# Two mixture layers in one kernel: slots of 128 rows with a fixed expert, or of two 64-row halves with an expert each

## The chip, the cores and the metric

The kernel runs on one core of one Trainium2 chip. The metric is the device time of one execution in microseconds (us); the runs shown of the kernel before are 1005.9 (median of three, 1003.83 to 1006.94). One more execution was recorded by the hardware profiler, and all durations below come from it.

The core has five engines with a queue of instructions each: TensorE (PE, matmuls; its weight loads are shown as PEld), VectorE (DVE), ScalarE (ACT), GpSimd (POOL, which here issues the indirect DMAs) and SyncE (SP, which issues most other DMAs). They wait for each other through semaphores. SBUF is the working memory of 128 partitions, PSUM the memory that matmuls write.

## The reference

2048 tokens (8 sequences of 256) of 512 numbers pass through two layers, everything in f32. The parts that the change touches are the two mixtures of experts, in which each token goes to 2 of 8 experts:

```python
# layer 0, after attention (the kernel uses one 512x512 matrix per expert)
logits = jnp.clip(xt @ gate_w.T, -50.0, 50.0)
top_w, top_idx = jax.lax.top_k(logits, TOP_K)
rw = jax.nn.softmax(top_w, axis=-1)
...
contrib = jax.ops.segment_sum((xg * vals).T, rows, num_segments=H)
out = xt @ W.T + contrib.T

# layer 1, after a linear layer with adapters
probs = jax.nn.softmax(x @ gate_w, axis=-1)
gate_score, gate_idx = jax.lax.top_k(probs, TOP_K)
gate_score = gate_score / jnp.sum(gate_score, axis=-1, keepdims=True)
...
h = jnp.einsum('th,ehi->eti', x, fc1_w) + fc1_b[:, None, :]
h = jax.nn.gelu(h, approximate=False)
y = jnp.einsum('eti,eih->eth', h, fc2_w) + fc2_b[:, None, :]
out = jnp.einsum('eth,te->th', y, combine)
```

So each layer has 4096 (token, expert) rows, and how many fall to each expert is known only at run time.

## The kernel before

The kernel does attention first (q, k, v products, a gathered cache, scores, L1176 to L1240), then the mixture of layer 0, the linear layer of layer 1 with its adapters (L1581 to L1632), and the mixture of layer 1. The instructions are written out for the whole program; a scheduler places them on each engine's queue, by priorities and by what they depend on, except where `keep_in_program_order` fixes an order. `in_a_row` keeps a list of matmuls together on PE.

**Slots.** A mixture is computed in slots of 128 rows, each of one expert. An expert with n rows takes n / 128 slots, rounded up, so at most 39 slots are needed (`NSLOT`). 36 of them (`NLIKELY`) always run; the last three stand in a branch that is taken when more than 36 are in use (L1543, L1755, with the number loaded at L306).

**Routing.** `top2` and a softmax give the chosen experts `sel` and the coefficients `coef` as tables over 16 groups of 128 tokens. `route` then works on DVE and PE: ranks of each row within its expert (matmuls pst, pn, prk, L143 to L151), the number of slots per expert (nb, boff, bend), for each token the two rows that it gets (row, rows), slot and place in the slot, and the expert of each slot (owner_i). The table of tokens per slot comes out of 32 small matmuls (pm, L250) of one-hot tables: hot (L243) and put (L221 to L233), both from DVE. Results are token_i, weight and owner_i. `routing_constants` makes the tables of constants that this needs, with iotas on POOL and conversions on DVE (L95 to L133); those of layer 1 are made right before the slots of layer 0 start.

**A slot of layer 0** (L1527): POOL gathers 128 rows by an indirect DMA (`fetched`, L328), three slots ahead; PE transposes them (`turned`, L341, pa) two slots ahead, and DVE copies them to SBUF (xsT, L343). Then four matmuls, one per 128 of the 512 inputs, with xsT as the stationary operand and the expert's matrix, 512 columns, as the moving one. Which expert it is stands in a register, which PE loads from owner_i for eight slots at a time (L316), with one register operation per matmul. ACT scales by weight (L1537), and POOL adds the rows to sums_d in memory by an indirect DMA (L348).

**A slot of layer 1**: gather and transposes as above; first product ph (L1697) with w1, a copy to SBUF (h, ACT, L1705), four transposes (pu, L1711), four Gelus with the bias b1 (hs, ACT, L1714), second product py (L1725) with w2, the bias b2 added on DVE (L1733), scaled (L1736), and added to the output (L348). In PE's queue the first product of slot s is followed by the second product of slot s-1, then the transposes of h of slot s and of the gathered rows of slot s+2. PE, ACT and DVE each hold the expert's number in registers.

In the attention, po (L1230) is a pair of products in which each writes 64 of the 128 partitions of one PSUM tile:

```python
in_a_row(
    lambda c=c, r=r: nc.tensor.matmul(
        po[r * HD : (r + 1) * HD, :],
        kvs[t + c][:, v0 + r * HD : v0 + (r + 1) * HD],
        pTs[r][:, c * P : (c + 1) * P],
...
    for c in range(3)
    for r in range(2)
)
```

Names used below: the outer product of layer 1's linear layer, pc (L1623), runs on PE beside the routing of layer 1; output_rows (ph, L402) beside that of layer 0; pgb (L1396) and pw (L1348) belong to the folding of the adapters.

Of the kernel before, what the change touches and what calls it, by code (L numbers as in the profile page):

```python
# [19 lines left out]
P = 128  # L20
# [12 lines left out]
NSLOT = 2 * N // P + E - 1  # L33
NLIKELY = (2 * N + E * P // 2) // P
# [15 lines left out]
HEAD_ORDER = [0, 2, 1, 3, 4, 6, 5, 7]  # L50


@with_exitstack
def two_layer_kernel(ctx: ExitStack, tc: tile.TileContext, io: dict, out: bass.AP):
# [35 lines left out]
    def routing_constants(pool, late=False):  # L90
# [43 lines left out]
        return earlier, ahead, same_e, below_e, count, tok, part  # L134

    def route(keep, pool, psum, consts, sel, coef, tag, beside=None):


        earlier, ahead, same_e, below_e, count, tok, part = consts
        flat_sel = sel.rearrange("p i e -> p (i e)")  # L140

# [9 lines left out]
        nc.tensor.matmul(prk2, tot.to_broadcast([P, P]), ahead, start=False, stop=True)  # L151
        nb_i = pool.tile([P, E], I32, name="nb_i")
        nc.vector.tensor_scalar(nb_i, pn, float(P - 1), None, ALU.add)
        nc.vector.tensor_scalar(nb_i, nb_i, 7, None, ALU.arith_shift_right)
# [10 lines left out]
        nc.vector.tensor_scalar(boff, boff, float(P), 1.0, ALU.mult, ALU.add)  # L165
        row = pool.tile([P, NT, E], F32, name="row")
        nc.vector.tensor_tensor(
            row, prk, boff[:, None, :].to_broadcast([P, NT, E]), ALU.add
        )
        nc.vector.tensor_tensor(row, row, sel, ALU.mult)  # L170

        rows = pool.tile([P, 2, NT], F32, name="rows")
# [3 lines left out]
        cf = pool.tile([P, 2, NT], F32, name="cf")  # L176
# [8 lines left out]
        rows_i = pool.tile([P, 2, NT], I32, name="rows_i")  # L185
        nc.vector.tensor_scalar(rows_i, rows, 1.0, None, ALU.subtract)
        rem_i = pool.tile([P, 2, NT], I32, name="rem_i")
        nc.vector.tensor_scalar(rem_i, rows_i, P - 1, None, ALU.bitwise_and)
        nc.vector.tensor_scalar(rows_i, rows_i, 7, None, ALU.arith_shift_right)
        rem = pool.tile([P, 2 * NT], F32, name="rem")  # L190
        nc.vector.tensor_copy(rem, rem_i.rearrange("p r i -> p (r i)"))
        slot = pool.tile([P, 2 * NT], F32, name="slot")
        nc.vector.tensor_copy(slot, rows_i.rearrange("p r i -> p (r i)"))
# [7 lines left out]
        ge = pool.tile([P, NSLOT, E], F32, name="ge", tag="wide")  # L201
        nc.vector.tensor_tensor(
            ge,
            count[:, :NSLOT, None].to_broadcast([P, NSLOT, E]),
            bend[:, None, :].to_broadcast([P, NSLOT, E]),
            ALU.is_ge,
        )
        owner = pool.tile([P, NSLOT], F32, name="owner")
        nc.vector.tensor_reduce(owner, ge, AX.X, ALU.add)
        owner_i = keep.tile([P, NSLOT], I32, name=f"owner_i_{tag}")  # L210
        nc.vector.tensor_scalar(owner_i, owner, float(E - 1), None, ALU.min)

        used_i = keep.tile([P, 1], I32, name=f"used_i_{tag}")
        nc.vector.tensor_copy(used_i, bend[:, E - 1 :])

        if beside:
            beside()

        full = [P, 2 * NT, NSLOT]
        put = pool.tile([P, 2 * NT, 2, NSLOT], F32, name="put", tag="wide")  # L220
        nc.vector.tensor_tensor(  # L221
            put[:, :, 0, :],
            slot[:, :, None].to_broadcast(full),
            count[:, None, :NSLOT].to_broadcast(full),
            ALU.is_equal,
        )
        nc.vector.tensor_tensor(
            put[:, :, 1, :],
            put[:, :, 0, :],
            cf.rearrange("p r i -> p (r i)")[:, :, None].to_broadcast(full),  # L230
            ALU.mult,
        )
        nc.vector.tensor_tensor(  # L233
            put[:, :, 0, :],
            put[:, :, 0, :],
            what.rearrange("p r i -> p (r i)")[:, :, None].to_broadcast(full),
            ALU.mult,
        )
        pm = psum.tile([P, 2, NSLOT], F32, name="pm", tag="route_b")
        STEP = 4  # L240
        for j in range(0, 2 * NT, STEP):
            hot = pool.tile([P, STEP, P], F32, name="hot", bufs=2)
            nc.vector.tensor_tensor(  # L243
                hot,
                rem[:, j : j + STEP, None].to_broadcast([P, STEP, P]),
                count[:, None, :].to_broadcast([P, STEP, P]),
                ALU.is_equal,
            )
            for k in range(STEP):
                nc.tensor.matmul(  # L250
                    pm.rearrange("p c s -> p (c s)"),
                    hot[:, k, :],
                    put[:, j + k].rearrange("p c s -> p (c s)"),
                    start=(j + k == 0),
                    stop=(j + k == 2 * NT - 1),
                )
        token_i = keep.tile([P, NSLOT], I32, name=f"token_i_{tag}")
        nc.vector.tensor_scalar(token_i, pm[:, 0, :], part, None, ALU.add)
        weight = keep.tile([P, NSLOT], F32, name=f"weight_{tag}")
        nc.vector.tensor_copy(weight, pm[:, 1, :])  # L260
        return token_i, weight, owner_i, used_i
# [42 lines left out]
    def in_use(used_i):  # L304

        return nc.values_load(  # L306
            used_i[0:1, 0:1],
            min_val=0,
            max_val=NSLOT,
            skip_runtime_bounds_check_because="it is a count of slots",  # L310
        )

    def owners(owner_i, engine, s0, end=NSLOT):

        n = min(8, end - s0)
# [7 lines left out]
        return {s0 + j: v for j, v in enumerate(have)}  # L323

# [12 lines left out]

    def turned(pool, psum, xs):
        pa = psum.tile([P, KC, P], F32, name="pa")
        for k in range(KC):  # L340
            nc.tensor.transpose(pa[:, k, :], xs[:, k * P : (k + 1) * P], ident)  # L341
# [1108 lines left out]
    with ExitStack() as ffn:  # L1450
# [8 lines left out]
        consts = routing_constants(tp)  # L1459
# [4 lines left out]
        coef0 = tp.tile([P, NT, E], F32, name="coef0")  # L1464
# [7 lines left out]
        routed0 = route(rp0, tp, ps_r, consts, sel, coef0, "l0", rows_beside)  # L1472
# [32 lines left out]
    consts1 = routing_constants(rdy, late=True)  # L1505

    with ExitStack() as ffn:
        sx = ffn.enter_context(tc.tile_pool(name="sx0", bufs=4))
        sw = ffn.enter_context(tc.tile_pool(name="sw0", bufs=2))
        ps_a = ffn.enter_context(tc.tile_pool(name="ps_a0", bufs=2, space=PSUM))  # L1510
        ps_y = ffn.enter_context(tc.tile_pool(name="ps_y0", bufs=3, space=PSUM))
        token_i, weight, owner_i, used_i = routed0
        AHEAD_ROWS = 3

        def run_slots(first, end):
            own = {}
            xs = {s: fetched(sx, h_d, token_i, s) for s in range(first, min(first + AHEAD_ROWS, end))}
            xT = {s: turned(sw, ps_a, xs.pop(s)) for s in range(first, min(first + 2, end))}
            for s in range(first, end):
                if (s - first) % 8 == 0:  # L1520
                    own.update(owners(owner_i, mybir.EngineType.PE, s, end))
                if s + AHEAD_ROWS < end:
                    xs[s + AHEAD_ROWS] = fetched(sx, h_d, token_i, s + AHEAD_ROWS)
                xsT = xT.pop(s)
                py = ps_y.tile([P, D], F32, name="py")
                for k in range(KC):
                    nc.tensor.matmul(  # L1527
                        py,
                        xsT[:, k, :],
                        delta[k // HK][:, k % HK, bass.ds(own[s], 1), :].rearrange(  # L1530
                            "p a d -> p (a d)"
                        ),
                        start=(k == 0),
                        stop=(k == KC - 1),
                    )
# [3 lines left out]
                if s + 2 < end:  # L1539
                    xT[s + 2] = turned(sw, ps_a, xs.pop(s + 2))  # L1540

        run_slots(0, NLIKELY)
        with tc.If(in_use(used_i) > NLIKELY):  # L1543
            run_slots(NLIKELY, NSLOT)

# [6 lines left out]
    with ExitStack() as cond:  # L1552
# [104 lines left out]
        coef1 = tp.tile([P, NT, E], F32, name="coef1")  # L1657
# [5 lines left out]
        token_i, weight, owner_i, used_i = route(rp, tp, ps_l, consts1, sel1, coef1, "l1")  # L1663
# [6 lines left out]
    with ExitStack() as moe:  # L1670
        sb = moe.enter_context(tc.tile_pool(name="sb", bufs=1, side="right"))
        sx = moe.enter_context(tc.tile_pool(name="sx", bufs=4))
        sw = moe.enter_context(tc.tile_pool(name="sw", bufs=2))
        ps_a = moe.enter_context(tc.tile_pool(name="ps_a", bufs=2, space=PSUM))
        ps_h = moe.enter_context(tc.tile_pool(name="ps_h", bufs=2, space=PSUM))
        ps_u = moe.enter_context(tc.tile_pool(name="ps_u", bufs=2, space=PSUM))
        ps_y = moe.enter_context(tc.tile_pool(name="ps_y", bufs=2, space=PSUM))

        b2 = sb.tile([P, E, D], F32, name="b2")
        nc.sync.dma_start(  # L1680
# [58 lines left out]
        def run_slots(first, end):  # L1739
# [3 lines left out]
            for s in range(first, end):  # L1743
# [6 lines left out]
                if s + 2 < end:  # L1750
                    xT[s + 2] = turned(sw, ps_a, xs.pop(s + 2))
# [92 lines left out]
```

## Time and profile before

| | us |
|---|---|
| runs shown, median of three | 1005.9 (1003.83 to 1006.94) |
| profiled execution | 1001.5 |
| its span, first to last instruction | 999.8 |
| slots of layer 0, on PE | 455.8 to 595.6 |
| slots of layer 1, on PE | 709.9 to 990.8 |
| mean granted PE clock | 0.959 of full speed |

The costliest groups of the page:

| line, engine | what | count | busy us | mean ns |
|---|---|---|---|---|
| L1697 PE | first product, layer 1 | 288 | 131.8 | 600 |
| L1527 PE | product, layer 0 | 288 | 130.5 | 597 |
| L1725 PE | second product, layer 1 | 288 | 129.6 | 592 |
| L341 PE | transposes of gathered rows | 288 | 44.9 | 281 |
| L1711 PE | transposes of h | 144 | 21.6 | 273 |
| L1714 ACT | Gelu | 144 | 41.0 | 367 |

How to read it: a matmul instruction of f32 appears as two in the trace, each with its own weight load (36 slots x 4 x 2 = 288); a transpose appears as one. The mean duration of a matmul runs from its start to its modelled end, with the way through the array; the next one starts earlier, so the price of one is the distance between starts, which the timeline shows. Idle time of an engine other than the one that sets the pace costs nothing.

### The profile page before, as it was taken

To read this page: it belongs to the slowest core of one execution; us is meant where nothing else is said; L and a number is where in the kernel's file an instruction comes from. 1 tells how busy PE (TensorE), PEld (TensorE's weight loads), DVE (VectorE), ACT (ScalarE), POOL (GpSimd) and SP (SyncE) were. 2 spreads that over 40 slices of the span, in tenths; PEclk is the share of its full clock that TensorE was granted. 3 is DMA by queue.
4 is the path that set the end of the run, shared out by engine and by line. 5 is a ranking of instruction groups with operands and counts; after the bars stand their busy time and mean duration, and the time that the engine had idled before them with its cause. 6 is when DMAs were issued, how large, how long until landed. Compare 5 with 4: busy or idle time off the path is not lost. (4 is left out here: it accounts for less than half of the span.)

```text
span 999.8 us, 13283 instructions
## 1 busy us (share of the span) xinstructions
PE 940.0 (94%) x4145; PEld 514.0 (51%) x4145; DVE 439.9 (44%) x1439; ACT 382.1 (38%) x944; POOL 367.1 (37%) x320
## 2 busy tenths in 40 slices
PE   6999889999999998889999998998699999999996
PEld 3555645556556565455444455453344454445542
DVE  5789698855946766652111113540122222222221
ACT  3677265645747589521111122311122222222221
POOL 2722655665363100415667640000333333333321
PEclk9899699999999999898999996999799999999998
DMA  6697494342423012528998769841433333333222
GB/s 188 206 318 264 129 307 116 98 108 73 139 54 96 22 45 63 212 95 295 339 243 164 134 84 293 322 160 74 158 67 64 63 64 61 72 65 64 55 33 38
DMA packets 75125, 136.08 MB, mean 136 GB/s; under 512 B 17693, under 2 KB 23325, under 8 KB 74928
## 3 DMA queue, kind: packets, MB, share of 16 engines
q0 software_dynamic: 25984, 45.26, 23.7%
q1 hardware_dynamic: 38496, 74.57, 21.6%
q10 hardware_dynamic: 10576, 15.39, 4.3%
q8 instruction: 36, 0.59, 0.2%
q14 instruction: 33, 0.27, 0.1%
HBM read 91.00 MB, written 53.61 MB: 145 GB/s over the span
## 5 line engine op out<-in xcount | busy, mean ns | idle before, releaser
L1697 PE MATMUL ph<-w,xsT 128*128 x288 | 131.8, 600 | 0.0
L1527 PE MATMUL py<-delta,xsT 128*128 x288 | 130.5, 597 | 0.4 <-DVE low_i L108 0.4
L328 POOL DMA_INDIRECT xs<-g_d,token_i_l x36 | 37.0, 1027 | 254.1 <-PE pa L341 150.5
L1725 PE MATMUL py<-w,hs 128*128 x288 | 129.6, 592 | 0.5 <-ACT hs L1714 0.5
L343 DVE COPY xsT<-pa 128x512 f32<-128x512 f32 x72 | 49.5, 687 | 156.7 <-PE pa L341 156.7
L1733 DVE TENSOR_TENSOR y<-py,b 128x512 f32<-128x512 f32 x36 | 24.9, 691 | 211.9 <-PE py L1725 211.9
L1207 ACT ACTIVATE s<-s,mx,roots 128x384 f32<-128x384 f32 x128 | 89.8, 705 | 12.5 <-DVE mx L1203 11.6
L1725 PEld LDWEIGHTS py<-w,hs 128*128 128x128 f32 x288 | 54.6, 190 | 69.2 <-issue 68.2
L1714 ACT ACTIVATE hs<-pu,b 128x128 f32<-128x128 f32 x144 | 41.0, 367 | 115.4 <-PE pu L1711 115.4
L1527 PEld LDWEIGHTS py<-delta,xsT 128*128 128x128 f32 x288 | 52.5, 192 | 53.5 <-issue 53.5
L1697 PEld LDWEIGHTS ph<-w,xsT 128*128 128x128 f32 x288 | 52.6, 193 | 52.7 <-issue 52.7
L348 POOL DMA_INDIRECT out<-y,token_i_l x36 | 57.0, 1584 | 48.3 <-DVE y L1736 35.5
L926 PE MATMUL pkv<-wkv,xb 128*128 128x512 f32 x128 | 66.0, 642 | 8.5 <-DMA wkv<-wqkvT 8.5
L1230 PE MATMUL po<-pT,kv 128*64 128x128 f32 x768 | 66.0, 283 | 7.3 <-ACT pT L1225 7.3
L1191 DVE CUSTOM_DVE_ANT_0 s<-ps,mask 128x384 f32<-128x384 f32 x128 | 67.1, 550 | 11.7 <-PE ps L1176 10.0
L1537 ACT ACTIVATE y<-py,weight_l 128x512 f32<-128x512 f32 x36 | 24.7, 687 | 124.2 <-PE py L1527 121.5
L348 POOL DMA_INDIRECT sums_d<-y,token_i_l x36 | 57.1, 1585 | 34.0 <-ACT y L1537 17.6
L1230 PEld LDWEIGHTS po<-pT,kv 128*64 128x64 f32 x768 | 46.0, 136 | 43.2 <-ACT pT L1225 35.9
L1705 ACT COPY h<-ph 128x512 f32<-128x512 f32 x36 | 21.1, 585 | 111.2 <-PE ph L1697 111.2
L1176 PE MATMUL ps<-KT,QT 64*128 64x384 f32 x256 | 59.2, 544 | 4.2 <-DVE mx L1191 4.1
L1225 ACT COPY pT<-pp 128x384 f32<-128x384 f32 x128 | 55.9, 478 | 16.4 <-PE pp L1221 15.6
L1221 PE MATMUL pp<-ident,s 128*128 128x128 f32 x384 | 59.7, 283 | 2.5 <-DVE s L1218 2.5
(353 smaller groups left out, 1491.1 us busy)
## 6 DMA issues: line engine op xcount, KB each, us to landing
delta_d<-spread SPq DMA_DIRECT2D x16, 512.0 KB, 4.2
raw<-delta_d SPq DMA_DIRECT2D x16, 512.0 KB, 4.0
w<-fc_w SPq DMA_DIRECT2D x8, 1024.0 KB, 17.7
w<-fc_w SPq DMA_DIRECT2D x16, 512.0 KB, 14.5
part<-sums_d SPq DMA_DIRECT2D x32, 256.0 KB, 4.9
xb<-xT SPq DMA_DIRECT2D x5, 1024.0 KB, 6.4
sums_d<-zero SPq DMA_DIRECT2D x18, 256.0 KB, 5.7
kv_new<-kvt ACTq DMA_DIRECT2D x16, 256.0 KB, 4.1
```

Source lines behind the costliest of these rows:

```text
L343: nc.vector.tensor_copy(xsT, pa)
L348: nc.gpsimd.indirect_dma_start(out=sum_d, out_offset=bass.IndirectOffsetOnAxis(ap=token_i[:, s : s + 1], axis=0), in_=y, in_offset=None, b ...
L926: nc.tensor.matmul(pkv, xb[:, k, cols], wkv[:, k, :], start=(k == 0), stop=(k == KC - 1),)
L1176: lambda r=r: nc.tensor.matmul(pss[r], QT[r * HD : (r + 1) * HD, m, t * P : (t + 1) * P], KT[r * HD : (r + 1) * HD, u, t * P : t * P + WU] ...
L1191: nc.vector.tensor_tensor_reduce(out=s, in0=pss[r], in1=mask[:, t, :], scale=1.0, scalar=NEG, op0=ALU.add, op1=ALU.max, accum_out=mx[:, r ...
L1207: nc.scalar.activation(ss[r], ss[r], AF.Exp, bias=mx[:, r : r + 1], scale=root[:, r : r + 1], accum_out=sm[:, r : r + 1],)
L1221: nc.tensor.transpose(pp[:, c * P : (c + 1) * P], s[:, c * P : (c + 1) * P], ident)
L1225: nc.scalar.copy(pT, pp)
L1230: lambda c=c, r=r: nc.tensor.matmul(po[r * HD : (r + 1) * HD, :], kvs[t + c][:, v0 + r * HD : v0 + (r + 1) * HD], pTs[r][:, c * P : (c + 1 ...
L1527: nc.tensor.matmul(py, xsT[:, k, :], delta[k // HK][:, k % HK, bass.ds(own[s], 1), :].rearrange("p a d -> p (a d)"), start=(k == 0), stop= ...
L1697: nc.tensor.matmul(ph, xsT[:, k, :], w1[:, k, bass.ds(own_pe[s], 1), :].rearrange("p a d -> p (a d)"), start=(k == 0), stop=(k == KC - 1),)
L1725: nc.tensor.matmul(py, hs[:, k, :], w2[k // HK][:, k % HK, bass.ds(own_pe[s], 1), :].rearrange("p a d -> p (a d)"), start=(k == 0), stop=( ...
```

## The change

A slot now is of one of two kinds, and a `Plan` per layer says at build time how many there are of each:

- **whole**: 128 rows of a fixed expert (8 in layer 0, one for each expert; 22 in layer 1, three or two for each). No register holds its number.
- **paired**: two halves of 64 rows. The second half's expert is fixed, that of the first half is found by the routing (owner_i has an entry per paired slot, and counts units of 64 rows). 26 in layer 0, 12 in layer 1.

Both plans have 34 slots. An expert's rows fill first the fixed halves, then the whole slots, then free first halves. Rows that find no place, and one of the two rows of a token whose rows would meet in one slot, are counted (`left_i`); if there are any, a branch routes them anew and runs four slots of the old kind, and in a branch inside it up to 39. The products of a paired slot are `multiplied` in two: 64 stationary columns each, the second half first, in a row. A whole slot of layer 1 makes its first product transposed (w1 stationary, xsT moving, 16 matmuls of 128 columns) and leaves out h and its transposes. In paired slots the Gelus are of 64 columns and the addition of b2 is split into two of 64 partitions. `routing_constants` gets five fixed numbers per expert, by iotas; those of layer 1 are made when slot 3 of layer 0 has been issued.

```diff
-NSLOT = 2 * N // P + E - 1
-NLIKELY = (2 * N + E * P // 2) // P
+HR = P // 2
+NREST = 2 * N // P + E - 1
+NFEW = 4
...
+class Plan:
...
+    PAIRED, FULL = 128 * HR, 256 * HR
+
+    def __init__(self, full, side):
+        self.full = [e for e in range(E) for _ in range(full[e])]
+        self.side = [e for e in range(E) for _ in range(side[e])]
+        self.F, self.D = len(self.full), len(self.side)
+        self.n = self.F + self.D
...
+PLAN0 = Plan([1] * E, [3] * 6 + [4] * 2)
+PLAN1 = Plan([3] * 6 + [2] * 2, [1] * 6 + [3] * 2)
...
+        fixed = None
+        if plan:
+            fixed_i = pool.tile([P, 5, E], I32, name="fixed_i")
...
+                    nc.gpsimd.iota(
+                        fixed_i[:, j, e:end],
...
+            fixed = pool.tile([P, 5, E], F32, name="fixed")
+            after(nc.vector.tensor_copy(fixed, fixed_i))
...
+    def route(keep, pool, psum, consts, plan, sel, coef, tag, beside=None):
...
+        have = pool.tile([P, E], F32, name="have")
+        nc.vector.tensor_tensor(have, pn, fixed[:, 1, :], ALU.subtract)
+        boff, bend = units(pool, keep, tag, consts, have, HR)
+        nc.vector.scalar_tensor_tensor(
+            boff, boff, float(HR), fixed[:, 4, :], ALU.mult, ALU.add
+        )
...
+        for j, step in ((0, fixed[:, 3, :]), (1, boff)):
+            past = row if j == 0 else far
+            nc.vector.tensor_tensor(
+                past, prk, fixed[:, j, None, :].to_broadcast(each), ALU.is_ge
+            )
+            nc.vector.tensor_tensor(
+                past, past, step[:, None, :].to_broadcast(each), ALU.mult
+            )
+        nc.vector.tensor_tensor(row, row, far, ALU.add)
+        nc.vector.tensor_tensor(row, row, prk, ALU.add)
...
+        twice = pool.tile([P, NT], F32, name="twice")
+        nc.vector.tensor_tensor(twice, slot[:, :NT], slot[:, NT:], ALU.is_equal)
+        nc.vector.scalar_tensor_tensor(
+            slot[:, :NT], twice, 128.0, slot[:, :NT], ALU.mult, ALU.add
+        )
...
+        left = keep.tile(both, F32, name=f"left_{tag}")
+        nc.vector.tensor_scalar(left, slot, plan.n - 0.5, None, ALU.is_gt)
+        leaves = pool.tile([P, 1], F32, name="leaves")
+        nc.vector.tensor_reduce(leaves, left, AX.X, ALU.add)
+        pl = psum.tile([P, 1], F32, name="pl", tag="route_a")
+        nc.tensor.matmul(pl, leaves.to_broadcast([P, P]), consts[8], start=True, stop=True)
+        left_i = keep.tile([P, 1], I32, name=f"left_i_{tag}")
+        nc.vector.tensor_copy(left_i, pl)
...
+    def multiplied(py, xT, weights, experts):
+
+        if len(experts) == 1:
...
+        in_a_row(
+            lambda k=k, h=h: nc.tensor.matmul(
+                py[h * HR : (h + 1) * HR, :],
+                xT[:, k, h * HR : (h + 1) * HR],
+                of_expert(experts[h])(weights(k)),
+                start=(k == 0),
+                stop=(k == KC - 1),
+            )
+            for k in range(KC)
+            for h in (1, 0)
+        )
...
-    consts1 = routing_constants(rdy, late=True)
...
+    def run_rest(left_i, places, run):
+
+        with tc.If(number(left_i, 2 * N) > 0):
...
+                    have = route_rest(mk, mp, ps, places, used_i)
+                run(*have, 0, NFEW)
+                with tc.If(number(used_i, NREST) > NFEW):
+                    run(*have, NFEW, NREST)
...
+                if plan and s < F:
+                    experts = [plan.full[s]]
+                else:
+                    j = s - F
+                    if j not in own:
+                        own.update(owners(owner_i, mybir.EngineType.PE, j))
+                    experts = [own[j]] + ([plan.side[j]] if plan else [])
...
+                multiplied(py, xT.pop(s), lambda k: delta[k // HK][:, k % HK], experts)
...
+                if beside and s == 3:
+                    beside()
...
+    slots0(
+        token_i, weight, owner_i, 0, PLAN0.n, PLAN0,
+        lambda: made.append(routing_constants(rdy, PLAN1, late=True)),
+    )
...
+            def first_half(s, xsT):
+                if plan and s < F:
+
+                    pu = ps_u.tile([P, KC, P], F32, name="pu")
+                    for c in range(KC):
+                        for k in range(KC):
+                            nc.tensor.matmul(
+                                pu[:, c, :],
+                                w1[:, k, plan.full[s], c * P : (c + 1) * P],
+                                xsT[:, k, :],
+                                start=(k == 0),
+                                stop=(k == KC - 1),
+                            )
+                    return pu
...
+                for k in range(KC):
+                    for j, e in enumerate(who):
+                        col = e * KC + k
+                        nc.scalar.activation(
+                            hs[:, k, j * n : (j + 1) * n],
+                            pu[:, k, j * n : (j + 1) * n],
+                            AF.Gelu,
...
+                for j, e in enumerate(who):
+                    rows = slice(j * n, (j + 1) * n)
+                    nc.vector.tensor_tensor(y[rows], py[rows], of_expert(e, rows)(b2), ALU.add)
...
+    slots1(token_i, weight, owner_i, 0, PLAN1.n, PLAN1)
+    run_rest(left_i, places, slots1)
```

## The prediction

> **What bounds the kernel now.** The chain of waits of this profile ends after 12 us of tail, so I read the engines' totals first, then the two stretches that the change rewrites, then the PE timeline inside them.
>
> ```profile
> PE 940.0 (94%) x4145; PEld 514.0 (51%) x4145; DVE 439.9 (44%) x1439; ACT 382.1 (38%) x944; POOL 367.1 (37%) x320
> ```
>
> Busy time of PE is no proof, since matmuls overlap; the stretches say more. Columns: busy us (and instructions) of PE, PEld, DVE, ACT, POOL, granted PE clock, DMA share, GB/s.
>
> ```profile
> 455.80:595.70 139.90, 139.80 (x424) 68.38 (x424) 25.63 (x46) 24.05 (x35) 88.13 (x67) 0.99 0.88 213
> 709.80:990.80 281.00, 280.43 (x857) 139.04 (x856) 62.36 (x106) 63.39 (x181) 87.83 (x67) 0.99 0.34 59
> ```
>
> These are FFN 0 (36 slots, 3.88 us each) and FFN 1 (36 slots). PE has no hole in either and runs at the full clock; nobody else is near full. So a slot costs what PE needs for it, and only PE work counts. The timeline of PE in one slot of FFN 1, then of FFN 0 (start, length with the pipeline's end, count):
>
> ```profile
> 800.55 0.60 PE L1711 MATMUL pu<-ident,h 128*128 128x128 f32 x4
> 800.98 0.60 PE L341 MATMUL pa<-ident,xs 128*128 128x128 f32 x4
> 801.42 3.60 PE L1697 MATMUL ph<-w,xsT 128*128 x8
> 804.86 3.60 PE L1725 MATMUL py<-w,hs 128*128 x8
> ...
> 480.16 3.60 PE L1527 MATMUL py<-delta,xsT 128*128 x8
> 483.60 0.60 PE L341 MATMUL pa<-ident,xs 128*128 128x128 f32 x4
> 484.03 3.60 PE L1527 MATMUL py<-delta,xsT 128*128 x8
> ```
>
> Differences of starts give the prices: a product of 8 passes over 512 columns 3.44 (0.43 a pass; an f32 matmul is two passes in the trace), four transposes 0.43 (0.109 each). Slot of FFN 1: 2 x 3.44 + 2 x 0.43 = 7.74, by 36 = 278.6. Slot of FFN 0: 3.87.
>
> **Does the new plan hold these tokens?** The router of the reference, evaluated on its own inputs, gives expert counts 542 416 510 556 504 526 508 534 in layer 0 and 542 526 490 492 520 543 510 473 in layer 1. Beyond the fixed places (320 or 384; 448) they need 25 of 26 free halves in layer 0 and 12 of 12 in layer 1, and following the ranks through the new formulas no token gets both of its rows in one slot. So nothing is left over, the rest branch is skipped, and each layer runs 34 slots instead of 36: layer 0 has 8 whole and 26 paired, layer 1 22 whole and 12 paired.
>
> **Part 1, paired slots.** Each of the 4 products becomes two with 64 stationary columns, writing partitions 64-127 and 0-63. In program order they stand one after the other; in turn they would cost 6.88 instead of 3.44. The trace has this form already: the attention's po (L1230), also two 64-column halves of one PSUM tile, 12 passes over 128 columns.
>
> ```profile
> 253.42 0.88 PE L1230 MATMUL po<-pT,kv 128*64 128x128 f32 x12
> 254.23 0.66 PE L1221 MATMUL pp<-ident,s 128*128 128x128 f32 x4
> 254.81 0.92 PE L1176 MATMUL ps<-KT,QT 64*128 64x384 f32 x4
> ```
>
> Twelve in turn would need 12 x 0.109 = 1.31; the next group starts 0.81 later. So they ran in six pairs (0.654), plus 0.156 that is fixed; the four transposes behind them take 0.58, that is 0.436 + 0.144. I read the fixed parts as the price of changing the array's form: about 0.095 of emptying and 0.05 of a weight load that nothing hides. There and back: **0.30**. A paired product so costs 3.44 as before, and every stretch of paired work between full-width work 0.30 more.
>
> Here a rule of the Trainium skill speaks against the change: "TensorE: Matmul & The Clock Gate", section "Measured speedup vs the span model", has three column tiles reach only 2.38x. At that efficiency (0.79) two tiles reach 1.59x, an estimate: a paired product 6.88 / 1.59 = 4.33. There are 26 + 24 paired products, so by the rule 50 x 0.89 = 44 us more than by the row. The row wins: same chip, same f32 form, and its loss is the fixed 0.30, which weighs less on 3.44 than on 0.65. Only its 128 columns differ from our 512.
>
> **Layer 0 sum.** Two slots fewer: -2 x 3.88 = -7.8. The transposes of slot s+2 stand between consecutive products, so 25 changes there and back: +7.5. **-0.3**: the layer gains nothing.
>
> **Part 2, whole slots of layer 1.** The transposed product has 16 matmuls, 32 passes over 128 columns with a new weight tile each, in place of ph (3.44) and pu's transposes (0.43). Bound below by the streaming alone, 0.107 a pass (3.43), above by the weight load's own recorded length, 0.19 a pass (6.1). The nearest row is pm (L250), with 128 weight columns and new weights every pass:
>
> ```profile
> 440.05 1.01 PE L250 MATMUL pm<-put,hot 128*128 128x78 f32 x8
> 440.90 0.27 PE L1348 MATMUL pw<-ident,aT 128*128 128x128 f32 x1
> ```
>
> 0.85 for 8 passes, 0.106-0.112 each, although only 78 columns stream: the loads follow each other without gap and the streaming hides under them. I take 0.111: 32 x 0.111 = 3.55. A whole slot then costs 3.55 + 3.44 + 0.43 = 7.42 against 7.74; by 22, -7.0. The copy h on ACT (585 ns) goes too, and hs now has the whole of the next first product (3.5) as cover against 1.14 for four Gelus.
>
> **Layer 1 sum.** 22 x 7.42 + 12 x 7.74 = 256.1. A paired slot's two products stand side by side (first half of s, second of s-1), so 12 to 13 changes, +3.8. 259.9 against 278.6: **-18.7**.
>
> **Part 3, routing.** The new tables add to DVE some 6 operations of 0.28, 8 of 0.17 and the count of left rows, and drop 0.5 from the narrower put: +3 to 4 us before pm. In layer 1 put was ready at 656.9 and pm ran at 663.4, but now stands three pc matmuls (2.6) earlier: just covered, +0.5 (0 to 3). In layer 0 put was ready at 432.4 and PE free for pm at 437.1: 4.7 of cover; if one more slow DVE operation (2.0 at L300) falls in, 1 to 2 come through. One pgb product (0.86) and the matmul of left rows (0.22) now stand ahead of the last pm. Against that, the constants of layer 1 leave POOL's queue ahead of the first gather (445.41 to 446.4, -1.0) and DVE's ahead of xsT (-0.4). **-0.3** (-1.5 to +3). They now run at slot 3 of FFN 0, on POOL (88 busy of 140) and DVE (26 of 140), with ten more small operations on POOL; queued behind them are gathers three slots ahead: nothing, or about 1 if that lead is gone.
>
> **Part 4, registers and branches.** Whole slots need no expert number. The loads of numbers now start inside a paired slot; PE's sequencer runs some 2.5 us ahead of the array, a load takes 0.3 to 0.9: nothing (uncovered 0.6 each, five in all). The skipped block now holds a routing and 39 slots instead of 3 slots. "Runtime: NRT & Kernel Launch", section "Instruction fetch mechanics", says that a taken branch out of the fetched window stalls for a fetch; the trace has its branches at 0.05 to 0.35 us, over short blocks. PE branches about 5 us ahead of its last matmul in layer 0, so only ACT's could show: +0.3 (0 to 2).
>
> **Part 5, the tail.** The last slot is paired: eight Gelus of 64 columns. Four of 128 take 1.14 (0.285 apart), and the copies of this trace shrink 0.8 ns an element, so 0.23 each, +0.7; the biased add is made twice, one 691 ns add more. **+1.4**. In other paired slots both hide under 7.7 us of PE. Two gathers and two scatters fewer on POOL's queue; SP's is as it was.
>
> **Sum.** -0.3 - 18.7 + 0.5 - 0.3 + 0.3 + 1.4 = **-17.1**. The profiled execution took 1001.5 us (span 999.8), so about 984.4; it lies 4.4 below the median of the runs shown, 1005.9, so there **989**.
>
> **Rivals.**
> - *The halves don't pair at 512 columns* (slower). Place: the 50 paired products. Fully in turn, +172, about 1161; at the rule's 1.59x, +44, about 1033. It decides from 17.1 / 50 = 0.34 a product, a pair of passes at 0.47 instead of 0.43. For it: two streams of 512 columns at once are not in this trace. Against: po's pairs show no slip over six steps.
> - *The weight loads of the transposed product are not hidden* (slower): 22 x 32 x 0.08 = +56, about 1045; it decides from 0.136 a pass. For it: the recorded 190 ns. Against: pm.
> - *Rows are left over*, the plan not doing what it says: one layer's rest is a routing of some 28 us (417 to 445 here) and four slots with their start, about +60, 1049. Against: the counts; for: layer 1's plan is exactly full, and expert 6 uses 62 of its last 64 places.
> - *Given back at the seams*: routing late by 3 in each layer, fetches after branches 3 to 4 each, tail 3: +14, about 1003, no change to be told.
>
> **Chances.** Forecast 0.84, its own range 982 to 997; pairing fails 0.06, loads exposed 0.03, rows left 0.02, seams 0.05. No change means within 0.3%, 3 us, about what a measurement of this kernel can tell. Faster 0.84, same 0.05, slower 0.11. For eight in ten: 980 (form changes cheaper than 0.30, or loads at the stream's 0.107) to 1000 (seams at their upper ends).
>
> **What would show it.** Right: 34 slots of L341 in each layer; paired products 3.4 to 3.5 from start to start of the next group, FFN 0 as long as before (139 to 140), a period of 4.17 in its paired part; FFN 1 near 261 with 7.4 and 8.0 periods. Wrong: a second scatter of slots behind either FFN, paired products over 3.8, the transposed product over 4.2, or PE idle ahead of pm.

## The result and the profile after

The changed kernel takes 993.23 us (median of 7 executions, 989.03 to 997.1), the kernel before in the same comparison 1003.83 (7, 1000.3 to 1009.96). The ratio is 0.9883, with a 95% interval of 0.9848 to 0.9919. So it is faster, as forecast, and inside the range, but by 8 to 15 us and not by the 17 of the sum. The profiled execution shows the same: a span of 991.5 against 999.8, that is -8.3. One execution of a later run (both_again) fell into a slower state of the core and is left out of its figures.

The totals of the page first, then the two stretches of the slots (busy us and instructions of PE, PEld, DVE, ACT, POOL; granted PE clock; DMA share; GB/s), both counted from the first product; the second ends where the last second product starts:

```profile
PE 924.4 (93%) x4917; PEld 524.8 (53%) x4917; DVE 451.3 (46%) x1479; ACT 371.7 (37%) x958; POOL 356.8 (36%) x332
```

```profile
456.47:596.18 139.71, 139.70 (x609) 53.56 (x608) 24.82 (x45) 22.67 (x33) 83.71 (x74) 0.99 0.83 206
718.29:977.05 258.76, 258.08 (x1425) 157.37 (x1425) 69.95 (x109) 51.87 (x191) 81.27 (x62) 0.99 0.34 62
```

FFN 0 is as long as before (139.71 against 139.80), FFN 1 is 18.4 shorter (277.2 before, counted in the same way). The timeline of PE in a paired slot of layer 0, a whole one of layer 1 and a paired one of layer 1 (start, length with the pipeline's end, count):

```profile
493.10 3.65 PE L532 MATMUL py<-delta,xsT 128*64 128x512 f32 x16
496.69 0.66 PE L545 MATMUL pa<-ident,xs 128*128 128x128 f32 x4
497.27 3.65 PE L532 MATMUL py<-delta,xsT 128*64 128x512 f32 x16
...
738.64 0.60 PE L545 MATMUL pa<-ident,xs 128*128 128x128 f32 x4
739.07 3.74 PE L1940 MATMUL pu<-xsT,w 128*128 128x128 f32 x32
742.65 3.60 PE L523 MATMUL py<-w,hs 128*128 128x512 f32 x8
...
895.75 0.66 PE L545 MATMUL pu<-ident,h 128*128 128x128 f32 x4
896.24 0.60 PE L545 MATMUL pa<-ident,xs 128*128 128x128 f32 x4
896.77 3.65 PE L532 MATMUL ph<-w,xsT 128*64 128x512 f32 x16
900.25 3.60 PE L532 MATMUL py<-w,hs 128*64 128x512 f32 x16
903.79 0.66 PE L545 MATMUL pu<-ident,h 128*128 128x128 f32 x4
```

Differences of starts: period in layer 0 497.27 - 493.10 = 4.17; transposed product 742.65 - 739.07 = 3.58; whole slot of layer 1 7.44; paired product 900.25 - 896.77 = 3.48; paired slot of layer 1 903.79 - 895.75 = 8.04.

So the slots do what the sum said. What is missing was given back elsewhere. The program between the two layers is the same in both kernels; here is how it starts, before and after. First PE before:

```profile
588.59 7.03 PE L1527 MATMUL py<-delta,xsT 128*128 x16
596.18 0.63 PE L1348 MATMUL pw<-ident,wc 128*128 128x128 f32 x4 [0.56 <-PEq L1543]
597.05 0.88 PE L1348 MATMUL pw<-ident,wc 128*128 128x128 f32 x6 [0.24 <-ACTq L1543]
597.76 1.06 PE L1423 MATMUL pgw<-gw,wn 128*128 128x8 f32 x8
...
606.03 1.06 PE L1581 MATMUL pt<-ident,part 128*128 128x128 f32 x4
```

and after:

```profile
589.09 7.09 PE L532 MATMUL py<-delta,xsT 128*64 128x512 f32 x32
600.96 2.36 PE L1556 MATMUL pw<-ident,wc 128*128 128x128 f32 x10 [4.79 <-PEq L1718]
604.08 1.88 PE L1631 MATMUL pgw<-gw,wn 128*128 128x8 f32 x8 [0.76 <-ACT wn L1557]
...
615.55 1.06 PE L1808 MATMUL pt<-ident,part 128*128 128x128 f32 x4
```

From the end of FFN 0 to the first transpose of the linear layer (pt) 10.4 us passed before, now 19.4; 1.2 of these 9.0 come back before the routing of layer 1. PE stands still for 4.79 behind its jump over the branch at L1718, and the ten pw behind it take 2.36, at half the clock (1.28 where the clock is full, below). ACT's timeline in the same place, before and after, shows a second wait:

```profile
595.71 0.69 ACT L1537 ACTIVATE y<-py,weight_l 128x512 f32<-128x512 f32 x1 [2.75 <-PEq L1543]
597.12 0.59 ACT L1349 COPY wn<-pw 128x512 f32<-128x512 f32 x1 [0.72 <-ACTq L1543]
```

```profile
596.27 0.69 ACT L1757 ACTIVATE y<-py,weight_l 128x512 f32<-128x512 f32 x1 [2.75 <-PE py L532]
603.44 0.58 ACT L1557 COPY wn<-pw 128x512 f32<-128x512 f32 x1 [6.48 <-DMA sums_d<-y,token_i_l]
```

The first wn, a copy of pw that pgw needs, started 1.4 us behind the scaling of the last slot before (597.12 behind 595.71). Now it comes 7.2 behind it, and what it waited for is a scatter of layer 0, on POOL's queue.

The account by stages, from the two profiled executions:

| stage | predicted | measured |
|---|---|---|
| up to the first matmul of layer 0's routing, not touched | 0 | +1.4 |
| routing of layer 0, to the first product | -0.3 | -0.7 |
| FFN 0 | -0.3 | -0.1 |
| end of FFN 0 to the routing of layer 1 | +0.3 | **+7.8** |
| routing of layer 1, to the first product | +0.5 | +0.1 |
| FFN 1, to the start of the last product, Gelus in | -18.0 | -18.4 |
| tail | +0.7 | +1.7 |
| sum | -17.1 | -8.3 |

I take the first row for chance: in the profiles of this study the first matmul of that routing (pst) starts anywhere from 415 to 426. Two kernels were profiled twice (below): their spans differ by 7.7 and 1.7 us, and the starts of their first product in layer 0 by 5.6 and 1.9, so most of the spread of single executions seems to arise up to there.

### The profile page after: what moved, and what is told of

It reads as the page before. It is cut to its first block, busy times and chain, and to the rows that moved or that the text cites. A ratio compares the mean times of both kernels' runs of the same rounds, so it can differ in the third digit from the quotient of the medians.

```text
span 991.5 us, 14493 instructions
## 1 busy us (share of the span) xinstructions
PE 924.4 (93%) x4917; PEld 524.8 (53%) x4917; DVE 451.3 (46%) x1479; ACT 371.7 (37%) x958; POOL 356.8 (36%) x332
## 5 line engine op out<-in xcount | busy, mean ns | idle before, releaser
L1982 DVE TENSOR_TENSOR y<-py,b 64x512 f32<-64x512 f32 (+1 forms) x46 | 31.7, 690 | 185.9 <-PE py L523 122.2
L1966 ACT ACTIVATE hs<-pu,b 128x64 f32<-128x64 f32 (+1 forms) x184 | 46.0, 347 | 186.6 <-PE pu L1940 145.2
L532 PE MATMUL py<-delta,xsT 128*64 128x512 f32 (+1 forms) x416 | 94.8, 599 | 0.0
L1415 ACT ACTIVATE s<-s,mx,roots 128x384 f32<-128x384 f32 x128 | 89.7, 704 | 12.2 <-DVE mx L1411 11.3
L1940 PE MATMUL pu<-xsT,w 128*128 128x128 f32 x704 | 84.1, 279 | 0.0
L1940 PEld LDWEIGHTS pu<-xsT,w 128*128 128x128 f32 x704 | 82.2, 196 | 0.4 <-issue 0.4
L523 PE MATMUL py<-w,hs 128*128 128x512 f32 x176 | 79.3, 594 | 0.0
L556 POOL DMA_INDIRECT sums_d<-y,token_i_l x34 | 53.9, 1585 | 32.4 <-ACT y L1757 13.5
L545 PEld LDWEIGHTS pa<-ident,xs 128*128 128x128 f32 x272 | 32.7, 145 | 52.5 <-issue 45.9
L610 PE MATMUL ph<-woT,oT 128*128 128x512 f32 x128 | 60.3, 621 | 0.3 <-DVE lg L1462 0.3
L1072 PE MATMUL pq<-wq,xb 128*128 128x512 f32 x128 | 60.1, 618 | 0.0
```

Of the source, the lines that this page charges most:

```text
L523: nc.tensor.matmul(py, xT[:, k, :], of_expert(experts[0])(weights(k)), start=(k == 0), stop=(k == KC - 1),)
L532: lambda k=k, h=h: nc.tensor.matmul(py[h * HR : (h + 1) * HR, :], xT[:, k, h * HR : (h + 1) * HR], of_expert(experts[h])(weights(k)), star ...
L556: nc.gpsimd.indirect_dma_start(out=sum_d, out_offset=bass.IndirectOffsetOnAxis(ap=token_i[:, s : s + 1], axis=0), in_=y, in_offset=None, b ...
L610: nc.tensor.matmul(ph, oTs[i // 2][:, k, (i % 2) * P : (i % 2 + 1) * P], woT[:, k, :], start=(k == 0), stop=(k == KC - 1),)
L1072: nc.tensor.matmul(pq, xcols[:, k, :], wq[:, k, :], start=(k == 0), stop=(k == KC - 1))
L1415: nc.scalar.activation(ss[r], ss[r], AF.Exp, bias=mx[:, r : r + 1], scale=root[:, r : r + 1], accum_out=sm[:, r : r + 1],)
```

## The experiments

**What the branch costs PE.** PE's jump took 0.25 us before and 3.9 now (columns: count, shortest, median and longest in ns, first and last start):

```profile
L1543 PEldq COMPARE_BRANCH  x1: 247/247/247, 590.5 to 590.5; - x1
...
L1718 PEldq COMPARE_BRANCH  x2: 3832/3878/3924, 592.7 to 978.8; - x2
```

The one of layer 0 starts 3.5 us ahead of the last product's end, so the matmuls that are already in the array's queue cover all but 0.4 of it. But PE's sequencer then executes one instruction (at 596.67) and stands still again, until 600.59. The Trainium skill, "Runtime: NRT & Kernel Launch", section "Instruction fetch mechanics", has code come in blocks of 256 instructions, and a jump out of the fetched window wait for one. In the built program, counted without its labels, the jump passes 1330 instructions and lands at number 7617, that is 193 of a block of 256 (the expectation, which had counted labels too, says 200). If a block ends right behind it, the second stall is the next block, which nobody had ordered yet. Instructions inside the skipped block move the landing:

```diff
-    def run_rest(left_i, places, run):
+    def run_rest(left_i, places, run, pad=0):
...
+                    if pad:
+                        pd = ps.tile([P, P], F32, name="pd")
+                        for _ in range(pad):
+                            nc.tensor.transpose(pd, ident, ident)
...
-    run_rest(left_i, places, slots0)
+    run_rest(left_i, places, slots0, pad=32)
```

> The changed kernel with 32 transposes more inside layer 0's skipped block (never executed). Behind that block the changed kernel's PE stands still from 596.2 to 600.9, and what follows runs at a granted clock of 0.50 where it ran at 0.94 before. Theory (code fetch): PE's jump lands 200 instructions into a block of 256, the jump itself costs a fetch of 3.9 us that the array's queue hides, and the next block, needed one instruction later, costs another 3.9 us that nothing hides. Moved 64 instructions on, the landing lies far from the end of a block: hole under 1.5 us, linear layer's stage (first pw to first pst) back from 52.1 to 48.5-50, in all -5 to -8 us against the changed kernel, near 986. Rival (the hole comes from the branch itself, from a semaphore or from the DMA of the folded weights): nothing changes, 993. Rival (clock gate without the hole): hole goes, but the stage stays at 52: -4.

Measured: 993.03 us (6 executions), 0.9896 of before (0.9859 to 0.9933): no gain. PE's timeline of this kernel tells why:

```profile
596.70 7.09 PE L532 MATMUL py<-delta,xsT 128*64 128x512 f32 x32
605.08 1.28 PE L1556 MATMUL pw<-ident,wc 128*128 128x128 f32 x10 [1.29 <-PEq L1718]
611.47 1.88 PE L1631 MATMUL pgw<-gw,wn 128*128 128x8 f32 x8 [5.11 <-ACT wn L1557]
```

The hole behind the jump is gone (1.29) and the ten pw run at full clock, but now pgw waits 5.11 for wn, and it starts 7.7 us behind the end of FFN 0, as in the changed kernel (7.9). So the fetch was there, and was not what the stage waited for last. My theory, as I had put it, fell.

**The cost of the jump alone**, in the kernel before:

```diff
         with tc.If(in_use(used_i) > NLIKELY):
-            run_slots(NLIKELY, NSLOT)
+            for _ in range(13):
+                run_slots(NLIKELY, NSLOT)
+            pa = ps_a.tile([P, KC, P], F32, name="pa")
+            for _ in range(110):
+                nc.tensor.transpose(pa[:, 0, :], ident, ident)
```

> The kernel before, whose layer 0 block is never executed, made 13 slot triples long plus 110 transposes, so that PE's jump passes 1406 instructions instead of 94 and lands just ahead of the end of a block of 256. Nothing else of the change is in it. Theory (code fetch): the hole behind FFN 0 grows from 0.8 to about 4.8 us and the stage behind it from 48.6 to about 52: +6 to +8 us over the kernel before, about 1011 where it takes 1003.8. Rival (the hole belongs to the new slots, semaphores or routing): no change from before within 1 us.

Measured: 1004.03 (22 executions), 0.9999 of before (0.9977 to 1.0021). PE's jump takes 3.85 us here too, all of it covered, and the next instructions follow without a stall. I had meant to land at the end of a block, but had counted the program's labels, which are no instructions; the landing was at 194 of 256. One instruction earlier (193) the changed kernel stalls behind it, here nothing does, which fits blocks that begin at 194. The run shows what the long block costs with a lucky landing: nothing that the time of the kernel can tell, though pt starts 11.3 behind FFN 0 where it was 10.4.

**What wn waits for.** In the built programs the first wn waits for PE and DVE alone before, and after the change for all eight DMA queue counts of POOL as well. The memory map says why. The scaled rows y of layer 0 have four buffers. Before they end at byte 111,360 of a partition, and wn begins at 112,224. After the change rp0 also keeps coef0 and the places of the rows for the branch, the slots' buffers lie 1,248 bytes higher, and the last y (110,560 to 112,608) reaches 736 bytes into wn (from 111,872). So wn must wait until the last y that used this place has been scattered, and it learns this from counts which POOL brings up to date behind its own branch: after the last scatter, a load of left_i, a jump that holds POOL for 2.7 us, and the landing of the scatters. That is done at 603.1. One buffer less takes the overlap away:

```diff
-                y = sx.tile([P, D], F32, name="y")
+                y = sx.tile([P, D], F32, name="y", bufs=3)
```

> The changed kernel with three instead of four buffers y in layer 0's slots. With four, the last of them reaches 736 bytes per partition into the place of wn (first copy of the folding behind FFN 0), so that wn waits until POOL, behind its own jump, has counted all scatters as landed (wn at 603.4, the first pgw at 604.1, 7.9 us behind the end of FFN 0; 2.1 before the change). Nothing else moves. Theory now (two stalls side by side, each hiding the other: PE's second code fetch to 600.9, and wn behind POOL to 603.4): taking one alone gains little, 0.5 to 2.5 us against the changed kernel's 993: pgw follows the ten pw directly at about 603.2, clock 0.5 as now. Rival (the overlap of addresses is the only cause): -6 to -8, 986.

> Both at once: three buffers y, and the 32 transposes in the skipped block that moved PE's landing away from a block's end. Two stalls side by side: now both are gone, the hole on PE is about 1.3 us, pgw starts some 3 us behind the end of FFN 0, the clock stays near full for the ten pw as before the change, and from the end of FFN 0 to the first pt 10.5 to 12 us pass instead of 19.4: 7 to 9 us less than the changed kernel, 984 to 986. Rival (the stage is bound by something else, such as the loads of part): no more than narrow alone.

Measured: narrow 993.61 (6), 0.9878 (0.9849 to 0.9906); both 988.9 (6), 0.985 (0.9812 to 0.9888). PE with both stalls taken away:

```profile
593.81 2.74 PE L532 MATMUL py<-delta,xsT 128*64 128x512 f32 x12
598.22 1.28 PE L1556 MATMUL pw<-ident,wc 128*128 128x128 f32 x10 [1.67 <-PEq L1718]
599.53 1.06 PE L1631 MATMUL pgw<-gw,wn 128*128 128x8 f32 x8
...
610.04 1.06 PE L1812 MATMUL pt<-ident,part 128*128 128x128 f32 x4
```

The stage in each kernel, in us behind the end of FFN 0 (each from its own profile):

| kernel | first pw | first pgw | first pt |
|---|---|---|---|
| before | 0.6 | 2.1 | 10.4 |
| changed | 4.8 | 7.9 | 19.4 |
| landing moved (shift) | 1.3 | 7.7 | 19.2 |
| no overlap (narrow) | 4.6 | 6.7 | 18.0 |
| both | 1.7 | 3.0 | 13.5 |

Each alone brings 0.2 and 1.4, both together 5.9: two stalls side by side, each hidden by the other. The forecast for both was 10.5 to 12 us to pt and 984 to 986; it came to 13.5 and 989. Against the kernel before 3.1 us are left: 0.9 until the first pgw, where PE's first fetch outlasts its cover by 1.1, and 2.2 between pgw and pt (10.5, before 8.3). For these the granted clock (the third figure from the end) of the stretch from the end of FFN 0 to pt speaks. Before, changed, and both:

```profile
595.60:606.10 10.50, 9.71 (x58) 8.66 (x58) 2.53 (x9) 3.46 (x7) 1.55 (x1) 0.77 0.70 154
```

```profile
596.18:615.60 19.42, 13.88 (x57) 12.69 (x58) 2.45 (x9) 3.56 (x7) 1.55 (x1) 0.58 0.55 150
```

```profile
596.50:610.10 13.60, 11.91 (x59) 10.82 (x58) 2.45 (x9) 3.56 (x7) 1.55 (x1) 0.65 0.67 166
```

The same matmuls (57 to 59 records) keep PE busy for 9.7, 13.9 and 11.9 us, the longer the lower the clock. The Trainium skill, "TensorE: Matmul & The Clock Gate", section "Part 1: The HAM clock gate", has the clock halve after an idle window of about 3.4 us that runs free of the program. The hole of 4.8 is longer than that, and the pw behind it run at 0.50; without the hole the clock still falls in this stretch, between 600 and 601 in "both" and between 601 and 602 before, where PE's longest gaps are 1.67 and 0.56. What decides the moment was not tried.

How much the clock takes shows in two kernels where it stays up for (nearly) all of this stretch: far, with 0.96, and the last one below (whole), which has this stage as in "both", with 1.00. This is whole, the stretch and then pt:

```profile
589.90:601.30 11.40, 7.48 (x59) 6.72 (x58) 2.38 (x10) 3.84 (x8) 1.55 (x1) 1.00 0.58 124
```

```profile
601.25 0.63 PE L1812 MATMUL pt<-ident,part 128*128 128x128 f32 x4 [2.56 <-DVE aTg L1647]
```

The same matmuls take 7.5 us, and pt starts 11.3 behind FFN 0 in both kernels, 2.2 ahead of "both": this part of the 3.1 is the clock. PE is no longer last there. It waits 2.6 (far: 3.0) for DVE, which adds up part until 0.14 ahead of pt (the line names aTg, the DVE instruction beside it), and the loads of part start only when POOL, behind its own jump, has brought its counts up to date: 7.0 (whole) and 7.1 (far) behind FFN 0, 3.7 in the kernel before. So a third bound stood behind the two stalls, 0.9 above the 10.4 of before.

Since the gain was not much larger than the intervals, the changed kernel and the one without the two stalls ran once more, on one chip:

> The changed kernel unaltered, beside the kernel with both stalls taken away, on one chip and against the same runs of before: the differences so far (989 against 993) are as large as the intervals. Both theories: 993, and 19 us from the end of FFN 0 to the first pt.

> Both stalls taken away, on the same chip as the unaltered one. Theory of two stalls: 4 to 8 us less than the changed kernel, 10.5 to 13.5 us from the end of FFN 0 to the first pt. Rival (the first measurement was chance): the same within 2 us.

Measured: 996.28 (6 executions, 986.49 to 1000.91) and 989.44 (5, 980.79 to 991.41), ratios to before 0.9876 (0.9834 to 0.9918) and 0.981 (0.9766 to 0.9854). From FFN 0 to pt 19.3 and 13.3. Over all 13 and 11 executions the means are 993.8 and 989.0, 4.8 apart. The stage repeats to 0.2 us, while single executions spread over 14.

**The two stalls in the kernel before**, without anything of the change:

```diff
-                y = sx.tile([P, D], F32, name="y")
+                y = sx.tile([P, D], F32, name="y", bufs=5)
...
-            run_slots(NLIKELY, NSLOT)
+            for _ in range(13):
+                run_slots(NLIKELY, NSLOT)
+            pa = ps_a.tile([P, KC, P], F32, name="pa")
+            for _ in range(109):
+                nc.tensor.transpose(pa[:, 0, :], ident, ident)
```

> The kernel before with nothing of the change but the two stalls: the never executed block of layer 0 made 1404 instructions long for PE, landing two instructions ahead of the end of a block, and five buffers y instead of four, so that the last overlaps wn. Theory: wn waits for POOL's count behind its jump (about 607.5 where PE ends FFN 0 at 600.5 in the kernel with the long block), PE idles, the clock falls: +6 to +9 us over the kernel before, about 1011. Rival (the given-back time belongs to the new slots or the new routing): no change from before.

Measured: 1012.15 (7), 1.007 of before (1.0044 to 1.0096). PE's timeline:

```profile
593.35 7.03 PE L1527 MATMUL py<-delta,xsT 128*128 x16
602.65 1.28 PE L1348 MATMUL pw<-ident,wc 128*128 128x128 f32 x10 [2.28 <-issue]
608.51 1.87 PE L1423 MATMUL pgw<-gw,wn 128*128 128x8 f32 x8 [4.58 <-ACT wn L1349]
...
619.98 1.06 PE L1585 MATMUL pt<-ident,part 128*128 128x128 f32 x4
```

19.6 us from FFN 0 to pt, as in the changed kernel. The landing is now at 192, and the stall is there (2.28 where it was 0.56 at 194; the jump starts 5.1 us ahead of the end of FFN 0 here, so more of the second fetch is covered). Two instructions are executed behind this landing and one behind that of the changed kernel, so the stalls stand ahead of numbers 7362 and 7618, exactly 256 apart. The loss is reproduced with the slots and the routing of before.

**The transposed product undone**, in whole slots of layer 1 alone:

```diff
             def first_half(s, xsT):
-                if plan and s < F:
+                if False:
...
             def middle(s, had):
-                if plan and s < F:
+                if False:
```

> The changed kernel with part 2 undone: whole slots of layer 1 make ph, its copy and four transposes again, in 34 slots. My sum: 22 whole slots at 7.74 instead of 7.42-7.45, so FFN 1 is 6.5 to 7 us longer than the changed kernel's (258.8 from first product to last py): about 265.4, total near 1000. Layer 0 and the hole behind it unchanged. Rival (weight loads exposed in the transposed product): FFN 1 no longer than now.

Measured: 1002.68 (20 executions), 0.9974 of before (0.9949 to 0.9999). FFN 1 takes 264.2 in its profile, 5.5 more than the changed kernel's (6.5 to 7 were expected); from the routing's first matmul on it is 7.3 (331.3 against 324.0), since the first product starts later. So part 2 is worth about 7 us, most of the gain that is left.

**What lets the halves run side by side.** Each paired product issues its matmuls in alternation. This kernel issues one half's four behind the other's:

```diff
-            for k in range(KC)
             for h in (1, 0)
+            for k in range(KC)
```

> The changed kernel with the order inside a paired product turned: all four matmuls of the second half, then all four of the first, instead of in alternation. Theory (halves run side by side only where their matmuls stand next to each other in the queue, since PE starts matmuls in order): a paired product takes nearly 6.9 instead of 3.44, 50 of them: +150 to +172, about 1150. Rival (each half of the array has its own queue and they find each other over eight passes): under +20.

Measured: 1059.61 (one execution). PE's timeline in layer 0:

```profile
583.60 5.42 PE L532 MATMUL py<-delta,xsT 128*64 128x512 f32 x16
588.95 0.66 PE L545 MATMUL pa<-ident,xs 128*128 128x128 f32 x4
589.54 5.42 PE L532 MATMUL py<-delta,xsT 128*64 128x512 f32 x16
```

Between the two forecasts: 588.95 - 583.60 = 5.35 for a product, where it is 3.59 in alternation and 6.9 was expected. The single records show the first pass of the second group starting 1.77 us behind the first of the first group, some four passes of 0.43; from there on both run side by side, the later group's passes ahead of passes that precede them in the program. It looks as if PE took up matmuls only about four passes ahead here; the alternation in the program is worth 1.76 us a product.

**A better plan.** If a change of form costs 0.30, whole slots are cheaper than paired ones in both layers, and the same 34 slots can have more of them: three for each expert, and ten paired. The counts allow it, with no row left over and no token twice in a slot. Besides the plans this kernel has both stalls removed (64 transposes of padding for its new landing):

```diff
-PLAN0 = Plan([1] * E, [3] * 6 + [4] * 2)
-PLAN1 = Plan([3] * 6 + [2] * 2, [1] * 6 + [3] * 2)
+PLAN0 = Plan([3] * E, [1] * 6 + [2] * 2)
+PLAN1 = Plan([3] * E, [1] * 6 + [2] * 2)
```

> As both, and with other plans of the same 34 slots: in each layer three whole slots for every expert and ten paired ones (before: 8 whole and 26 paired in layer 0, 22 and 12 in layer 1), the landing again away from a block's end. If a change of form costs 0.30 there and back, layer 0 loses 16 of them, -4.8, and layer 1 two slots of 8.04 for two of 7.44, -1.2: 6 us less than both, 978 to 980. Rival (the paired part's period of 4.17 is not from the changes of form but from gathers or scatters): layer 0 as long as now.

Measured: 981.55 (6 executions, 979.4 to 985.64), 0.9768 of before (0.9739 to 0.9796). FFN 0 takes 135.9 against 140.7 in the kernel "both": 4.84 for 16 changes there and back, 0.302 each. FFN 1 is 1.3 shorter, as expected; another 1.9 comes from the stage between the layers, where the clock falls later than in "both". This is the fastest kernel of the study, about 24 us faster than before and some 12 faster than the changed one. Its price is a demand on the router: an expert with fewer than 384 rows leaves whole slots partly empty, and the branch then has to take more.

## Why the prediction was right, and where it was off

- **What bounds the kernel** (a slot costs what PE needs for it): right in both layers. FFN 0 and FFN 1 are still without a hole, at a clock of 0.99.
- **Nothing left over**: right. 34 gathers and 34 scatters in each layer, and no second scatter of slots behind either.
- **Paired slots**: right. 3.48 for a paired product against the 3.44 forecast, 4.17 for the period, 0.30 for a change of form (0.302 by the whole-slot plan). The rule of the skill that spoke against it (4.33 at the efficiency of three column tiles) doesn't hold for these two 64-column tiles: 6.88 / 3.48 = 1.98. The rival that the halves don't pair is out, but its mechanism exists: with the order turned they gain only 6.88 / 5.35 = 1.29.
- **Layer 0 sum -0.3**: -0.1. **Layer 1 sum -18.7**: with the Gelus -18.0 forecast, -18.4 measured. The transposed product took 3.58, not 3.55; the rival of exposed weight loads is out.
- **Routing +0.5 and -0.3**: +0.1 and -0.7, inside their bounds.
- **Registers and branches, +0.3 (0 to 2)**: this is the term that failed. The stage behind it became 7.8 us longer. I read only the records of the jumps over short blocks (0.05 to 0.35) and argued that "PE branches about 5 us ahead of its last matmul in layer 0, so only ACT's could show". It branches 3.5 ahead, which covers the one fetch (3.9) but for 0.4; but a landing just ahead of a block's end brings a second one, uncovered. And the sum had no term at all for the memory map: rp0 keeps more, the slots' buffers move up, and the first copy behind FFN 0 gets a new wait on POOL. The rival of the seams, +14 "given back", had the right place for a part of it (fetches, 3 to 4 each), at a chance of 0.05. It lacked the overlap and the clock. Of the two stalls, neither is worth much without the other. The total still fell into the range because the range was wide, 982 to 997, and not because this term held.
- **Tail +1.4**: +0.2 for the eight Gelus (1.34 us from the last transposes to py, 1.12 before), not 0.7, because the product's first matmuls need only the first two Gelus and the rest follow under it; +0.7 for the second biased add, as forecast; and +1.1 that I did not have, from the issue of the last scatter to the end of the span (983.73 to 991.5, before 993.12 to 999.8), where POOL has its own jump (2.6, before 0.2). I have not tried that last one alone.

## What to carry to other kernels

When a change keeps more tables alive, look at which buffers move, and which instructions then gain waits: a copy with eight new DMA waits on its list costs more than the tables did. A branch that is never taken is not free. Count how many instructions each engine jumps over and where it lands, ask what covers the fetch, and expect that taking one of two stalls away shows next to nothing until the other one is gone too.

## What the hardware showed beside this

- A jump over 1,330 to 1,460 instructions holds PE's sequencer for 3.4 to 4.6 us in the profiles here, the one over some 2,400 at the end of layer 1 for 3.4 to 4.8, so the length adds next to nothing; jumps over some 90 and 170 take 0.25 and 0.35. A landing one or two instructions ahead of the end of a block of 256 stalls again behind it (changed kernel and farlap); moved by 64 instructions (shift), or onto a block's first instruction (far), it doesn't.
- Behind the jump over the long block POOL goes on 2.5 to 3.0 us later, behind the short one 0.2 to 0.5, and whoever waits for its DMA counts waits along: wn in the changed kernel, part in far and whole.
- Two 64-column f32 matmuls with 512 moving columns run side by side almost without loss when they alternate in the program (3.48 us against 3.44 for one full-width product), and lose 1.76 us of 3.59 when four of one half stand ahead of four of the other: only some four of twelve pass times are then shared (5.35 / 0.43 = 12.4). Matmuls of the two halves start out of program order there.
